# Two of the sixteen blocks of a partition exchange become copies on GpSimd and ScalarE

## The chip, the core and the metric

The kernel runs on one core of one Trainium2 chip. A core has a matrix engine (TensorE, PE in the profile, with its weight loads shown as PEld), three engines for elementwise work (VectorE = DVE, ScalarE = ACT, GpSimd = POOL), and a queue engine (SyncE = SP) which in this kernel does nothing but issue DMA transfers. Each engine takes its instructions strictly in the order in which the program lists them; engines wait for each other through semaphores. The metric is the device time of one execution in microseconds, as a median over runs.

## The reference

The computation is one layer of a transformer block on `x` with 8 batches of 512 rows of 256 values. First comes gated cross-attention, then a gated mixture of experts:

```
x = x + tanh(g_xattn) * (softmax(scale * q k^T) v  Wo + bo)      # 16 heads of 64, 512 keys
        q = layernorm(x) Wq,  k = ctx Wk,  v = ctx Wv
x = x + tanh(g_ffn) * sum over 2 chosen of 8 experts of weight_e * (layernorm(x) We + be)
```

All of it is float32. For every batch and head the attention needs the 512 x 512 matrix of probabilities twice in different orientations: the softmax wants a query's keys along the free dimension, and the product with `v` wants the keys on the partitions.

## The kernel before

**Units and steps.** Heads are taken in pairs (`hp` = 0 to 7), and the 512 queries in four tiles of 128 (`nt` = 0 to 3). One *unit* is (batch, pair, tile). The main loop goes through *steps* of two units, so a pair takes two steps and a batch sixteen: pair `hp` of batch `b` has its first two units in step 16b + 2hp (an even step) and its last two in step 16b + 2hp + 1 (an odd step). There are 128 such steps and some more behind them.

**What a unit goes through.** `scores` (L378, PE) makes 128 queries x 512 keys for each of the two heads in PSUM. `unit_max` (DVE) takes the row maxima (`nm`, L389) and scales them (`nb`, L392, a tiny instruction on 128 x 2 values). `unit_exp` (L401, ACT) writes the exponentials `p` and their sums, `unit_norm` (L410 on DVE, `rs`; L412 on POOL) multiplies them by the reciprocal of the sums. One step later `unit_T` (L425, DVE) transposes `p` in blocks of 32 x 32 into the tile `tt`.

**The exchange.** A transpose of 32 x 32 blocks is not yet a transpose of 128 x 512: the blocks must also move between the four groups of 32 partitions. `exchange` (L433 to L442) does this once per pair, after the last of its four units has been transposed, so in step 2hp + 2 of its batch. It is a list of sixteen DMA transfers, `PAIRS`: block (q, a) goes from partition group `a` of `tt` to partition group `q` of the tile `pt`, 32 partitions x 1024 values (128 KB) each. The first four of the list have q = a: source and target lie in the same 32 partitions. All sixteen go out on SP (in the very last exchange every second one goes out on ACT's queue).

**Who uses it.** `values` (L453, PE, sixteen matmuls `av`) multiplies `pt` by `v` in step 2hp + 5 of the batch. `tt` and `pt` have two buffers each, so the transposes of pair hp + 2, which begin in the same step 2hp + 5, reuse the `tt` of pair hp and wait for its exchange as well.

**The order.** Every function is planned for a step; within a step the scores and maxima of the step come first, and all other functions follow in the order of the list `SCHED["order"]`, which holds for every engine's queue. In it `unit_exp0` comes early, `values` in the second half and `exchange` is next to last. Projections of q, k and v (L357, L367, L347), the output projection (L471) and the expert matmuls are planned for even steps (`at` moves them there), `values` comes in odd steps. So ACT's queue ends an even step with the copies `v`, `k` and `q` out of PSUM (L351, L368, L361) and begins the odd one with the exponentials. POOL also carries `x<-x,tgbo` (L333, a bias on a whole batch tile of x, once per batch), the reciprocal root of the variance (`rstd`, L262), the layer norm of the second half (`xn_f`, L269) and the indirect DMAs of the expert sorting (L611, L733, L793). SP also carries the loads of x, of its transpose and of the context, and the stores and loads of the sorting.

Of the kernel before, what the change touches and what calls it, by code (L numbers as in the profile page):

```python
# [43 lines left out]
        "lt": 2, "lm": 4, "cn": 1, "lc": 2, "lo": 3,  # L44
    },
    "order": [
        "center_q", "sum_q", "ranks_mm", "keep_out", "keep_y", "ln_T", "expert_bias",
        "unit_exp0", "out_proj", "unit_T0", "clear_lists", "logits", "load_lists", "plan4",
        "unit_T1", "places", "ln_apply", "route1", "unit_exp1", "plan1", "plan2", "plan1b",
        "plan3", "load_batch", "sort_setup", "ranks", "experts", "unit_norm0", "values",  # L50
# [9 lines left out]
def kernel(  # L60
# [17 lines left out]
    nc = tc.nc  # L78
# [6 lines left out]
    NT = N // P  # L85
# [102 lines left out]
    def late_setup():  # L188

        nc.sync.dma_start(out=wo_sb, in_=wo.rearrange("(c p) d -> p c d", p=P))  # L190
        nc.sync.dma_start(out=gw_sb, in_=gate_wT.rearrange("(k p) e -> p k e", p=P))
        for k in range(KD):
            nc.sync.dma_start(
                out=we_sb[:, k].rearrange("p (e o) -> p e o", o=O),
                in_=expert_wT[:, :, ts(k, O)].rearrange("e p o -> p e o"),
            )
        nc.gpsimd.memset(eb2, 0.0)
        for t in range(NT):
            nc.sync.dma_start(out=eb2[32 * t : 32 * t + E, ts(t % 2, O)], in_=expert_b)
        nc.scalar.activation(tg, gts, AF.Tanh)  # L200

        nc.gpsimd.tensor_scalar(tgbo, bo_bc, tg[:, 0:1], 1.0, ALU.mult, ALU.mult)

        for e in range(E):
            nc.gpsimd.memset(rev[:, :, e : e + 1], float(E - e))

        for cg in cgs:
            nc.gpsimd.memset(cg, 0.0)
# [104 lines left out]
    def first_q(h):  # L313

        if h == 0:
            qs[0, 0] = qkp.tile([P, N], F32, tag="q", name="q_0_0")
        w = N // 2
        pq = ps_m.tile([P, 512], F32, tag="m", name=f"pq_0_0_{h}")[:, :w]
        for k in range(KD):
            nc.tensor.matmul(  # L320
                pq, lhsT=wq_sb[:, k, ts(0, P)], rhs=xTs["q", 0][:, k, ts(h, w)],
                start=(k == 0), stop=(k == KD - 1),
            )
        nc.scalar.copy(qs[0, 0][:, ts(h, w)], pq)
# [6 lines left out]
    def add_bias(b):  # L331

        nc.gpsimd.tensor_tensor(  # L333
            xs[b], xs[b], tgbo.unsqueeze(1).to_broadcast([P, NT, D]), ALU.add
        )
# [3 lines left out]
    ks, vs, probs, tts, pts, aos = {}, {}, {}, {}, {}, {}  # L339
# [34 lines left out]
    def scores(b, hp, nt):  # L374
        q, kt = qs[b, hp], ks[b, hp]
        sc = ps_s.tile([P, 2, M], F32, tag="s", name=f"sc_{b}_{hp}_{nt}")
        for j in range(2):
            nc.tensor.matmul(  # L378
                sc[:, j, :], lhsT=q[ts(j, HD), ts(nt, P)], rhs=kt[ts(j, HD), :],
                start=True, stop=True,  # L380
            )
        return sc
# [3 lines left out]
    def unit_max(u, sc):  # L386

        nm = small.tile([P, 2], F32, tag="nm", name="nm_%d_%d_%d" % u)
        nc.vector.tensor_reduce(nm, sc, AX.X, ALU.max, negate=True)  # L389
        rstd = lns["q", u[0]][2][:, u[2] : u[2] + 1]  # L390
        nb = small.tile([P, 2], F32, tag="nb", name="nb_%d_%d_%d" % u)
        nc.vector.tensor_scalar(nb, nm, rstd, 1.0, ALU.mult, ALU.mult)  # L392
        maxes[u] = (sc, nb, rstd)
# [36 lines left out]

    PAIRS = [(q, (q + d) % 4 if d % 2 == 0 else q ^ d) for d in (0, 1, 2, 3) for q in (0, 2, 1, 3)]

    def exchange(b, hp):  # L433
        tt = tts.pop((b, hp)).rearrange("p (q k) t l -> p q (k t l)", q=4)
        pt = ptp.tile([P, 4, 2, MT, NT * 32], F32, tag="pt", name=f"pt_{b}_{hp}")
        pts[b, hp] = pt
        last = (b, hp) == (B - 1, NP_ - 1)
        for i, (q, a) in enumerate(PAIRS):
            (nc.scalar if last and i % 2 else nc.sync).dma_start(  # L439
                out=pt[ts(q, 32), a].rearrange("i j r n -> i (j r n)"),  # L440
                in_=tt[ts(a, 32), q],
            )  # L442

    def values(b, hp):
        pt = pts.pop((b, hp))
        v = vs[b, hp // 2]
        ao = aop.tile([P, N], F32, tag="ao", name=f"ao_{b}_{hp}")
        aos[b, hp] = ao
        av = ps_m.tile([P, N], F32, tag="m", name=f"av_{b}_{hp}")
        for mt in range(MT):  # L450
            for j in range(2):
                c = (hp % 2) * P + j * HD
                nc.tensor.matmul(  # L453
                    av[ts(j, HD), :],
                    lhsT=v[:, mt, c : c + HD],
                    rhs=pt[:, :, j, mt, :],
                    start=(mt == 0), stop=(mt == MT - 1),
                )
        nc.scalar.copy(
            ao.rearrange("p (t a l) -> p a t l", a=4, l=32),  # L460
            av.rearrange("p (a t l) -> p a t l", a=4, l=32),
        )
# [457 lines left out]
    for g, (b0, b1) in enumerate(GROUPS):  # L920
# [9 lines left out]
        r = 0  # L930
        for i in range((NTILES[g] + 1) // 2):
            r = G["fe"] + i * num // den
# [29 lines left out]
    def units(s):  # L962
        b, r = divmod(s, NS)
        return [(b, r // 2, 2 * (r % 2) + i) for i in range(2)] if 0 <= b < B else []

    order = {name: i for i, name in enumerate(SCHED["order"])}
    for s in range(max(plan) + 1):
        side = list(plan.get(s, []))
        for i, u in enumerate(units(s)):
            side.append((unit_exp, (i, u)))  # L970
            side.append((unit_norm, (i, u)))
        for i, u in enumerate(units(s - 1)):
            side.append((unit_T, (i, u)))
            if u[2] == NT - 1:
                side.append((exchange, u[:2]))
        scs = [scores(*u) for u in units(s)]
        for u, sc in zip(units(s), scs):
            unit_max(u, sc)
        if s == 0:
            first_q(1)  # L980
            late_setup()
            add_bias(0)
        name = lambda f: f[0].__name__ + (str(f[1][0]) if f[0] in (unit_exp, unit_norm, unit_T) else "")
        for fn, args in sorted(side, key=lambda f: order[name(f)]):
            fn(*args)
# [38 lines left out]
```

## Time and profile before

| | us |
|---|---|
| median of 3 runs | 1049.74 (1046.6 to 1052.07) |
| profiled execution, its own time | 1048.78 |
| its span, first to last instruction | 1046.8 |
| PE busy | 998.3 (95%) |
| DVE busy | 879.9 (84%) |
| ACT busy | 580.0 (55%) |
| POOL busy | 581.9 (56%) |

The span is that of one profiled execution; instruction times below are microseconds from its start. Matmuls are pipelined and their ends are modelled, so a matmul row of 602 ns each does not mean that one takes that long when they follow each other: sixteen `av` take 3.65 us together. A wait is written as the idle time of an engine before an instruction and the thing that ended it. Where an instruction waits for several things, the last of them is named, and sometimes that is only a neighbour that finished at the same moment. The exchange is the group `pt<-tt`: 1016 transfers on SP and 8 on ACT's queue, 134 of the 188.39 MB that the DMA engines move.

### The profile page before, as it was taken

How to read it: one execution, taken by the hardware profiler on the slowest of the kernel's cores; microseconds unless marked ns; L12 is line 12 of the kernel's file. 1: busy time of each engine (PE TensorE's matmuls, PEld its weight loads, DVE VectorE, ACT ScalarE, POOL GpSimd, SP SyncE). 2: the span in 40 equal slices, each digit the busy share in tenths (PEclk: the TensorE clock that was granted, in tenths of full speed). 3: DMA queues.
4: the chain of work that ended last, by engine and by line, in shares of the span. 5: the costliest groups of instructions: out<-in, count | busy, mean ns of one | idle time of the engine just before them, and what ended most of it. 6: DMA issues, size and time to landing. Idle time of an engine off the chain costs nothing.

```text
span 1046.8 us, 14817 instructions
## 1 busy us (share of the span) xinstructions
PE 998.3 (95%) x4024; PEld 492.5 (47%) x4024; DVE 879.9 (84%) x1604; ACT 580.0 (55%) x1379; POOL 581.9 (56%) x771
## 2 busy tenths in 40 slices
PE   8899999999999999989899999999999998898998
PEld 5335344534454444435353445546465543454653
DVE  5998989998999989998899999866686789985467
ACT  4666666566565656575646665665655755552110
POOL 4544546445753466455644665756765457876432
PEclk9999999999999999999999999999999999999999
DMA  7787777769766787576776787787777677889433
GB/s 257 164 202 191 167 177 188 185 146 174 190 158 164 181 192 181 145 179 157 179 175 145 169 194 197 188 205 205 189 192 184 164 146 193 224 226 247 151 118 110
DMA packets 93328, 188.39 MB, mean 180 GB/s; under 512 B 22880, under 2 KB 52992, under 8 KB 93248
## 3 DMA queue, kind: packets, MB, share of 16 engines
q1 hardware_dynamic: 85216, 170.90, 66.5%
q0 software_dynamic: 6816, 14.45, 5.4%
q10 hardware_dynamic: 1216, 2.10, 0.7%
q8 instruction: 34, 0.56, 0.3%
q14 instruction: 46, 0.38, 0.1%
HBM read 33.99 MB, written 19.16 MB: 51 GB/s over the span
## 4 chain that ended last, share of the span: by engine, by line
PE 65%; DVE 17%; DMA 5%; SPq 5%; ACT 4%; issue 3%; DVEq 0%; ACTq 0%; POOL 0%; POOLq 0%
PE sc L378 15%; PE av L453 14%; PE po L471 8%; PE pq L357 8%; DVE nm L389 5%; SPq L439 5%; DMA pt<-tt 5%; DVE tt L425 4%; PE py L761 4%; ACT p L401 4%; PE pv L347 4%; PE pk L367 3%; PE pe L839 3%; DVE nb L392 3%; PE pl L492 1%
## 5 line engine op out<-in xcount | busy, mean ns | idle before, releaser
L401 ACT ACTIVATE p<-sc,nb,rstd_q 128x512 f32<-128x512 f32 x512 | 391.5, 774 | 282.1 <-DVE nb L392 255.4
L412 POOL TENSOR_SCALAR p<-p,rs 128x512 f32<-128x512 f32 x512 | 345.4, 690 | 359.2 <-DVE rs L410 354.4
L389 DVE TENSOR_REDUCE nm<-sc 128x2 f32<-128x1024 f32 x256 | 314.3, 1228 | 67.9 <-PE sc L378 50.5
L425 DVE STREAM_TRANSPOSE tt<-p 128x1024 f32<-128x1024 f32 x256 | 303.9, 1222 | 9.6 <-DMA pt<-tt 7.4
L378 PE MATMUL sc<-k,q 64*128 64x512 f32 x1024 | 261.4, 624 | 19.0 <-ACT p L401 13.4
L453 PE MATMUL av<-pt,v 128*64 128x512 f32 x1024 | 235.5, 602 | 12.3 <-DMA pt<-tt 7.9
L378 PEld LDWEIGHTS sc<-k,q 64*128 64x128 f32 x1024 | 85.9, 186 | 179.7 <-issue 102.1
L453 PEld LDWEIGHTS av<-pt,v 128*64 128x64 f32 x1024 | 70.0, 137 | 170.6 <-issue 145.8
L357 PE MATMUL pq<-xT_q,wq_sb 128*128 128x512 f32 x252 | 120.0, 598 | 3.7 <-DVE wq_sb L309 1.3
L471 PE MATMUL po<-wo_sb,ao 128*128 128x256 f32 x512 | 118.8, 385 | 0.0
L471 PEld LDWEIGHTS po<-wo_sb,ao 128*128 128x128 f32 x512 | 94.7, 190 | 30.6 <-issue 18.2
L392 DVE TENSOR_SCALAR nb<-nm,rstd_q 128x2 f32<-128x2 f32 x256 | 96.4, 376 | 9.2
L401 ACT ACTIVATION_READ_ACCUMULATOR p<-sc,nb,rstd_q 128x1 f32 x512 | 102.0, 199 | 0.0
L357 PEld LDWEIGHTS pq<-xT_q,wq_sb 128*128 128x128 f32 x252 | 47.8, 192 | 67.4 <-issue 57.3
L793 POOL DMA_INDIRECT yg<-ysort,back x48 | 46.6, 971 | 52.3 <-PE xgt L750 19.1
L733 POOL DMA_INDIRECT xg<-xn_d,rows x62 | 61.5, 992 | 15.1 <-issue 13.7
L347 PE MATMUL pv<-wv_sb,ctxT 128*128 128x256 f32 x256 | 68.8, 391 | 0.9 <-issue 0.9
L367 PE MATMUL pk<-ctxT,wk_sb 128*128 128x512 f32 x128 | 66.5, 602 | 2.1 <-DVE x L475 2.1
L761 PE MATMUL py<-we_sb,xgT 128*128 x248 | 57.2, 380 | 3.1 <-DVE x L846 3.1
L347 PEld LDWEIGHTS pv<-wv_sb,ctxT 128*128 128x128 f32 x256 | 45.9, 191 | 23.7 <-issue 18.7
L839 PE MATMUL pe<-we_sb,xT_f 128*128 128x512 f32 x128 | 57.0, 595 | 0.0
L611 POOL DMA_INDIRECT list<-lin,ai x48 | 49.8, 1038 | 10.5 <-issue 10.0
(131 smaller groups left out, 730.7 us busy)
## 6 DMA issues: line engine op xcount, KB each, us to landing
pt<-tt SPq DMA_DIRECT2D x1016, 128.0 KB
ysort<-y SPq DMA_DIRECT2D x30, 256.0 KB
x<-in_x SPq DMA_DIRECT2D x8, 512.0 KB
xT_q<-in_xT SPq DMA_DIRECT2D x7, 512.0 KB
xn_d<-xn_f SPq DMA_DIRECT2D x6, 512.0 KB
x1d<-x SPq DMA_DIRECT2D x5, 512.0 KB
acc<-x1d SPq DMA_DIRECT2D x20, 128.0 KB
out<-acc SPq DMA_DIRECT2D x20, 128.0 KB
```

Source lines behind the costliest of these rows:

```text
L347: nc.tensor.matmul(pv[:, r, :], lhsT=cts[b][:, ts(2 * h + r, P)], rhs=wv_sb[:, ts(g, 2 * P)], start=True, stop=True,)
L357: nc.tensor.matmul(pq, lhsT=wq_sb[:, k, ts(hp, P)], rhs=xTs["q", b][:, k, :], start=(k == 0), stop=(k == KD - 1),)
L367: nc.tensor.matmul(pk, lhsT=wk_sb[:, ts(hp, P)], rhs=cts[b], start=True, stop=True)
L378: nc.tensor.matmul(sc[:, j, :], lhsT=q[ts(j, HD), ts(nt, P)], rhs=kt[ts(j, HD), :], start=True, stop=True,)
L389: nc.vector.tensor_reduce(nm, sc, AX.X, ALU.max, negate=True)
L392: nc.vector.tensor_scalar(nb, nm, rstd, 1.0, ALU.mult, ALU.mult)
L401: nc.scalar.activation(p[:, :, j, :], sc[:, j, :].rearrange("p (q c) -> p q c", q=4), AF.Exp, bias=nb[:, j : j + 1], scale=rstd, accum_out ...
L412: nc.gpsimd.tensor_scalar(p[:, :, j, :], p[:, :, j, :], rs[:, j : j + 1], 1.0, ALU.mult, ALU.mult)
L425: nc.vector.transpose(tts[b, hp][:, :, nt, :], p.rearrange("p q j c -> p (q j c)").rearrange("p (k l) -> p k l", l=32),)
L453: nc.tensor.matmul(av[ts(j, HD), :], lhsT=v[:, mt, c : c + HD], rhs=pt[:, :, j, mt, :], start=(mt == 0), stop=(mt == MT - 1),)
L471: nc.tensor.matmul(po, lhsT=aos[b, c][:, ts(t, P)], rhs=wo_sb[:, c, :], start=(i == 0), stop=(i == HC - 1),)
L761: nc.tensor.matmul(py[:, a, :], lhsT=xt[:, k, a, :], rhs=we_sb[:, k, bass.ds(col[a], O)], start=(k == 0), stop=(k == KD - 1),)
```

## The change

Blocks (0, 0) and (1, 1) of each exchange are no longer transfers. A new function `stay` copies them: GpSimd copies block (1, 1), ScalarE block (0, 0), each 32 partitions x 1024 values. It is planned one step after the exchange (step 2hp + 3 of the batch, an odd step) and stands first in the order, so in ACT's and POOL's queues it precedes everything else of that step. `exchange` keeps the `tt` tile for it. The other fourteen blocks stay as they are.

```diff
     "order": [
-        "center_q", "sum_q", "ranks_mm", ...
+        "stay", "center_q", "sum_q", "ranks_mm", ...
...
+    STAY = [(1,), (0,)]
+
     def exchange(b, hp):
-        tt = tts.pop((b, hp)).rearrange("p (q k) t l -> p q (k t l)", q=4)
+        tt = tts[b, hp].rearrange("p (q k) t l -> p q (k t l)", q=4)
         pt = ptp.tile([P, 4, 2, MT, NT * 32], F32, tag="pt", name=f"pt_{b}_{hp}")
         pts[b, hp] = pt
         last = (b, hp) == (B - 1, NP_ - 1)
         for i, (q, a) in enumerate(PAIRS):
+            if q == a and q in STAY[0] + STAY[1]:
+                continue
             (nc.scalar if last and i % 2 else nc.sync).dma_start(
                 out=pt[ts(q, 32), a].rearrange("i j r n -> i (j r n)"),
                 in_=tt[ts(a, 32), q],
             )
+
+    def stay(b, hp):
+        tt = tts.pop((b, hp)).rearrange("p (q k) t l -> p q (k t l)", q=4)
+        for copy, qs_ in zip((nc.gpsimd.tensor_copy, nc.scalar.copy), STAY):
+            for q in qs_:
+                copy(pts[b, hp][ts(q, 32), q].rearrange("i j r n -> i (j r n)"), tt[ts(q, 32), q])
...
+        for u in units(s - 2):
+            if u[2] == NT - 1:
+                side.append((stay, u[:2]))
```

More of the change, by code (lines that the diff above doesn't have):

```diff
@@ L46 @@
     "order": [
-        "center_q", "sum_q", "ranks_mm", "keep_out", "keep_y", "ln_T", "expert_bias",
+        "stay", "center_q", "sum_q", "ranks_mm", "keep_out", "keep_y", "ln_T", "expert_bias",
         "unit_exp0", "out_proj", "unit_T0", "clear_lists", "logits", "load_lists", "plan4",
```

## Prediction

> **What bounds the kernel now.** I read the page first (engine shares), then the chain that ended last, then the waits of PE, then the timeline around single steps, and last the groups by form for the price of a copy.
>
> ```profile
> PE 998.3 (95%) x4024; PEld 492.5 (47%) x4024; DVE 879.9 (84%) x1604; ACT 580.0 (55%) x1379; POOL 581.9 (56%) x771
> PE 65%; DVE 17%; DMA 5%; SPq 5%; ACT 4%; issue 3%; DVEq 0%; ACTq 0%; POOL 0%; POOLq 0%
> ...
> PE sc L378 <- ACT p L401: 13.4, 13, 2.5
> PE av L453 <- DMA pt<-tt: 7.9, 6, 3.0
> PE av L453 <- DVE nb L392: 2.2, 2, 1.4
> PE av L453 <- DMA li<-list: 1.4, 1, 1.4
> PE av L453 <- DVE nm L389: 0.8, 1, 0.8
> ```
>
> PE is the bound, and it is nearly always at work. The chain's DMA and SPq shares (5% each, some 100 us) look like a large prize, but they count all the time in which the chain runs through the exchange, while PE did other work beside it. What PE really loses before the first `av` is the four `av` rows: 7.9 + 2.2 + 1.4 + 0.8 = 12.3 us, in ten places. The last three rows are the same wait under a neighbour's name, since `av` waits for `pt` alone besides long finished things. In the other 54 pairs the exchange is in time and a shorter one gains nothing.
>
> The ten waits, from the timeline of PE (start of `av`, idle before): 42.3, 0.94; 66.1, 0.41; 133.0, 1.13; 257.2, 0.82; 285.0, 2.21; 354.5, 0.85; 466.9, 1.37; 510.0, 2.98; 596.7, 1.39; 855.9, 0.19.
>
> **Part 1, two transfers fewer.** An undisturbed exchange shows SP's price:
>
> ```profile
> 597.10 10.04 SPq L439 DMA_DIRECT2D pt<-tt  x16
> ...
> 510.02 5.28 PE L453 MATMUL av<-pt,v 128*64 128x512 f32 x16 [2.98 <-DMA pt<-tt]
> ```
>
> 10.04 / 16 = 0.63 us each, so the last block is issued 1.25 us earlier and, other things equal, lands that much earlier. Each of the ten waits shrinks by the smaller of itself and 1.25: 0.94 + 0.41 + 1.13 + 0.82 + 1.25 + 0.85 + 1.25 + 1.25 + 1.25 + 0.19 = 9.3. One is not worth it: behind the `av` of 285.0 the second pair of score matmuls starts at 289.59, 0.19 after the second unit's exponentials end (289.40), because `nb` was held 2.95 us there; PE would wait for ACT instead. That takes the 1.25 down to 0.1: **8.2 us**. For the other nine the scores behind `av` start 0.7 to 2.6 us after the exponentials they need, so the gain passes on. The `av` at 510.0 also takes 5.28 us where others take 3.65, at a granted clock of 0.94 in 490 to 520; if a 1.7 us wait no longer brings that, 1.6 more. I count half: **0.8**. Bounds: nothing if what lands last is set by other traffic, 12.3 + 1.6 = 13.9 if all ten waits vanish. I take the middle, since an issue interval is what the 1.25 is made of.
>
> SP is moved past nothing, it loses 128 issues (80 us). The DMA engines lose 16.8 of 188.39 MB.
>
> **Part 2, the copy on ACT.** 32 x 1024 values. Nearest rows: COPY 128x512 at 588 to 603 ns, 128x256 at 372 to 390; so 0.8 ns a value, and 590 + 512 x 0.8 = 1.0 us, plus a semaphore wait of 0.04. It is queued ahead of the exponentials, after the `q` copy of the even step:
>
> ```profile
> 494.10 0.58 ACT L361 COPY q<-pq 128x512 f32<-128x512 f32 x1 [1.13 <-PE pq L357]
> 496.78 0.78 ACT L401 ACTIVATE p<-sc,nb,rstd_q 128x512 f32<-128x512 f32 x1 [2.09 <-DVE nb L392]
> ...
> 493.52 2.69 POOL L412 TENSOR_SCALAR p<-p,rs 128x512 f32<-128x512 f32 x4 [3.38 <-DVE rs L410]
> 496.19 1.04 POOL L262 TENSOR_TENSOR rstd_f<-ve_f,mhalf 128x4 f32<-128x4 f32 x1
> ...
> 496.43 0.23 DVE L392 TENSOR_SCALAR nb<-nm,rstd_q 128x2 f32<-128x2 f32 x1
> ```
>
> ACT is idle for 2.09 us at this place, waiting for `nb`. The copy's own input (the transposes of the even step) ended at 493.37, before the `q` copy, so it does not wait. Over the 62 odd steps the room is 2.0 or more in 43, about 1.0 to 1.9 in the others but three, where it is 0.6 (121, 186, 636), where the exponentials come 0.45 late; there the next scores have 0.55 or more to spare. **0** on PE; if that cover were gone, 3 x 0.45.
>
> **Part 3, the copy on POOL.** Nearest rows: COPY 128x8 186 ns and CAST 128x40 217 (0.97 ns a value from one to the other), TENSOR_SCALAR 128x256 482 and 128x512 690 (0.82). 690 + 512 x 0.82 = **1.1 us**. Ends: MEMSET 128x512 514 ns, so 0.9; TENSOR_TENSOR 128x1024 2.36. I stay near the copies' own rows, which are the same kind of instruction.
>
> It starts right behind the four L412 of the even step (496.21 above), ahead of `rstd`, L333, L269, L611 and the indirect DMAs. The next L412 come 2.1 to 8 us later, and POOL has the 1.1 us free except once (668.7: 4.84 us with 4.36 of other work, so 0.6 late).
>
> What it hits is `nb`. This row shows it:
>
> ```profile
> 218.39 2.36 POOL L333 TENSOR_TENSOR x<-x,tgbo 128x1024 f32<-128x1024 f32 x1
> ...
> 218.93 1.85 DVE L392 TENSOR_SCALAR nb<-nm,rstd_q 128x2 f32<-128x2 f32 x1
> ...
> 222.58 1.13 PE L378 MATMUL sc<-k,q 64*128 64x512 f32 x4 [0.98 <-ACT p L401]
> ```
>
> A `nb` of 0.23 us takes until the POOL instruction beside it ends (220.75). Laying the `nb` starts of the odd steps over a 1.1 us copy behind the last L412: in nine steps (as above at 496.43) the first `nb` starts 0.2 to 0.3 us into it and both `nb` come 0.72 later; in fifteen the second starts some 0.5 into it and comes 0.45 later; elsewhere none falls into it. Against that, the scores of the next step start 0.62 (nine steps) or 0.25 to 1.6 (fifteen) after the exponentials they need. What exceeds this is 0.08 x 9 and 0.03 to 0.1 x 6, and 1.0 at 669.9, where L333 follows: **2.1 us lost**. That supposes that `nb` gets its turn when the copy ends; in the trace it did at 69 of 71 joins of one L412 with the next, and not at four joins of L269 with L412 (the 2.95 us).
>
> The page SBUF — State Buffer of the Trainium skill, section Who interferes with whom, says that VectorE in a two-port mode and GpSimd exclude each other for a whole instruction and that the first to start wins. It agrees with the 1.85 us and speaks against this change; taken alone, 62 copies of 1.1 us would cost 68 us, while the rows give 2.1 because most `nb` start elsewhere and PE has slack.
>
> The same effect gains where L333 follows L412 directly (218.39, 330.3, 442.1, 556.8): the copy comes first, `nb` slips in at its end, 1.2 us earlier than now, and L333 runs beside the transposes. PE's idle 0.98 before the second scores goes: 4 x 1.0 = **4.0 gained**. If `nb` misses its turn there, 4 x 1.1 lost.
>
> **Part 4, waits added.** The first transpose of pair hp + 2 and `av` wait for ACT and POOL as well, both done two steps before. A semaphore wait on DVE costs 0.1 us (62 x 0.1 beside slack), on PE 0.05; I take **1.0** for all.
>
> **Sum.** 8.2 + 0.8 + 4.0 - 2.1 - 1.0 = 9.9 us. Not all lasts: in 300 to 350, 425 to 450 and 550 to 600 DVE is busy 96% and sets the pace, and the two gains at 330 and 442 and the wait at 597 lie in or beside these. I keep three quarters, 7.5. The profiled execution's own time of 1048.78 becomes 1041.3; it stands 1.0 below the median, so 1042.3 against that.
>
> **Rivals.** *The gain is absorbed* (no measurable change): `av` is earlier, but PE then waits for ACT (already 13.4 us in 13 places) or DVE. For it: DVE at 84%, and the 285.0 case. Against: slack of 0.7 or more behind nine of ten waits. Of 9.9 a quarter stays: 1047. *The landing is not set by the issue*: at 510.0 the last block was issued 4.6 us before `av` could start, against about 2 in quiet places, so other traffic held it; then the change does not do what it says in the worst waits. Left: 0.94 + 0.41 + 1.13 + 0.82 + 0.19 + 4.0 - 3.1 = 4.4, three quarters 3.3: 1046.4. *GpSimd holds `nb` longer* (slower): the same laying over with a copy of 1.4 us costs 5.7 on PE, 1.7 us 11.7, 2.36 us 32; or with 1.1 us and every `nb` that is in the last L412 missing its turn, 12.9. It decides from 1.6 us on, where the cost passes the gain; in the middle of these it is 22 - 9 = 13 slower, 1063, with missed turns alone about 1054.
>
> **How the numbers follow.** The forecast has 0.56, its own range 1035 to 1046. The two absorbed cases together 0.25 (1045 to 1050). GpSimd 0.19 (1052 to 1068). About 0.5%, 5.2 us, is what a measurement can tell from no change: below 1044.5 is most of the forecast's share, 0.53; above 1055 or so are two thirds of the GpSimd case and a few strays, 0.17; the rest 0.30. The range leaves out one in ten at each side: 1033 (more waits vanish than 1.25 each, 13.9 + 4.0 - 1 = 17 off) to 1056.
>
> **What would show it.** Right: 888 `pt<-tt` on SP, exchanges of 8.8 us, the four `av` rows down to 3 or 4 us, an ACT COPY `pt<-tt` near 1.0 and a POOL COPY near 1.1 us, `nb` 1.2 us shorter at 219. Wrong: a POOL COPY over 1.6 us; `nb` over its 96.4 us by more than 20; the row of scores waiting for `p` grown by what the `av` rows lost.

## The result and the profile after

The changed kernel takes 1115.72 us (1111.77 to 1119.45) against 1050.07 us for the one before on the same chip: a ratio of 1.0604, with a 95% interval of 1.0573 to 1.0634. The change costs 65.7 us; 7.5 us of gain were forecast, and the range ended at 1056.

The profiled execution has a span of 1113.5 us. Four lines of its page: the engines, the granted clock in 40 slices of the span (9 is 90% or more), and two groups (busy time and mean ns of one, then the idle time before them and what ended most of it).

```profile
PE 1024.1 (92%) x4024; PEld 497.9 (45%) x4024; DVE 888.9 (80%) x1604; ACT 641.9 (58%) x1443; POOL 648.0 (58%) x835
...
PEclk9899999998999999999999999999999988898999
...
L425 DVE STREAM_TRANSPOSE tt<-p 128x1024 f32<-128x1024 f32 x256 | 306.7, 1226 | 94.9 <-POOL p L412 84.6
...
L452 POOL COPY pt<-tt 32x1024 f32<-32x1024 f32 x64 | 65.8, 1028 | 150.3 <-DMA pt<-tt 73.8
```

Two of VectorE's groups before, for comparison:

```profile
L425 DVE STREAM_TRANSPOSE tt<-p 128x1024 f32<-128x1024 f32 x256 | 303.9, 1222 | 9.6 <-DMA pt<-tt 7.4
...
L392 DVE TENSOR_SCALAR nb<-nm,rstd_q 128x2 f32<-128x2 f32 x256 | 96.4, 376 | 9.2
```

The single instruction is hardly slower: a transpose takes 1226 ns (1222 before), a GpSimd copy 1028; `nb` as a group grew from 96.4 to 107.1 us. What is new is idle time. GpSimd stands idle for 150.3 us in front of its copies, and VectorE for 84.6 us in front of its transposes, waiting for a norm (L412) of GpSimd. PE's own 4024 instructions have become 25.8 us longer (998.3 before) at a mean granted clock of 0.974 instead of 0.993, so part of the loss lies in PE's own rows and not in its waits.

The list of waits shows who waits (engine, tile and line, what ended the wait: us in total, times, longest):

```profile
DVE tt L425 <- POOL p L412: 84.6, 25, 8.5
...
POOL pt L452 <- DMA pt<-tt: 73.8, 12, 11.1
...
PE sc L378 <- ACT p L401: 38.3, 37, 4.3
...
POOL pt L452 <- DMA list<-lin,ai: 7.4, 1, 7.4
```

The first two rows did not exist before. `pt<-tt` in the second is a neighbour's name: the exchange of the same pair is still running when these copies start, so the copy does not wait for it. The last row gives the real one away, an indirect write of the lists. Of the 64 copies 33 start within 0.2 us of the instruction ahead of them; the other 31 stand idle for 148 us together. All 31 lie behind the first indirect DMA of GpSimd (240.73 us).

The first such place, GpSimd's timeline and VectorE's:

```profile
244.23 2.69 POOL L412 TENSOR_SCALAR p<-p,rs 128x512 f32<-128x512 f32 x4 [2.25 <-DVE rs L410]
247.09 1.06 POOL L621 DMA_INDIRECT list<-lin,ai  x1 [0.17 <-issue]
259.23 1.03 POOL L452 COPY pt<-tt 32x1024 f32<-32x1024 f32 x1 [11.08 <-DMA pt<-tt]
260.35 2.02 POOL L412 TENSOR_SCALAR p<-p,rs 128x512 f32<-128x512 f32 x3
```

```profile
251.61 1.22 DVE L389 TENSOR_REDUCE nm<-sc 128x2 f32<-128x1024 f32 x1
...
261.74 2.58 DVE L425 STREAM_TRANSPOSE tt<-p 128x1024 f32<-128x1024 f32 x2 [6.90 <-POOL p L412]
```

GpSimd issues an indirect write of a list (1.06 us), and then the copy, next in its queue, does not start for 11.08 us. Its input was finished at 244.07. The norms stand behind the copy, and the transposes need the norms: VectorE idles 6.90 us, and the maxima, exponentials and scores behind it are late. In the trace the last indirect write ahead of the copy lands at 258.94, 0.3 us before the copy starts. Each such place adds some us that nothing gives back: the last transpose of pair 15 ends at 228.2 us before and 231.4 after, that of pair 31 at 452.0 and 469.3, of pair 47 at 678.6 and 706.9, of pair 63 at 950.7 and 1016.7.

Why the copy waits is in the instruction list of the built program. Around this place it reads (numbers are places in GpSimd's queue; the first buffer number of a name is left out; a list ends with the semaphores, that is the counters, that the instruction waits for):

```
209 L621 DMACopy list_1_156<-lin,ai_2122 16384x1
210 L452 TensorCopy pt_0_2380<-tt_0_2299 32x1024 [waits DMAHW2_49,DMAHW3_49,DMAHW1_49,DMAHW4_49,DMAHW0_49,DMAHW5_49,DMASW1_49,DMAHW6_49,DMASW0_49,DMAHW7_49,PE_49,Pool_49]
211 L412 TensorScalarPtr p_1_2_2411<-p_1_2_2411,rs_1_2_2422 128x4x128 [waits DVE_49,Pool_49]
```

The DMAHW and PE entries are the old users of this `pt` buffer, long done. DMASW0 and DMASW1 are the counters of the indirect DMAs that GpSimd has issued itself since its last copy: here the writes of two lists, which have no byte in common with `pt` or `tt`. Pool_49 is GpSimd's own counter: the copy also waits for the GpSimd instructions ahead of it. Of the 64 copies 38 carry a DMASW entry. It was in the program before any run; my prediction did not ask for it.

### The profile page after: what moved, and what is told of

Same layout as the page of the kernel before. It is cut to its first block, busy times and chain, and to the rows that moved or that the text cites. A ratio compares the mean times of both kernels' runs of the same rounds, so it can differ in the third digit from the quotient of the medians.

```text
span 1113.5 us, 15502 instructions
## 1 busy us (share of the span) xinstructions
PE 1024.1 (92%) x4024; PEld 497.9 (45%) x4024; DVE 888.9 (80%) x1604; ACT 641.9 (58%) x1443; POOL 648.0 (58%) x835
## 5 line engine op out<-in xcount | busy, mean ns | idle before, releaser
L412 POOL TENSOR_SCALAR p<-p,rs 128x512 f32<-128x512 f32 x512 | 344.7, 689 | 214.3 <-DVE rs L410 187.3
L425 DVE STREAM_TRANSPOSE tt<-p 128x1024 f32<-128x1024 f32 x256 | 306.7, 1226 | 94.9 <-POOL p L412 84.6
L378 PE MATMUL sc<-k,q 64*128 64x512 f32 x1024 | 273.4, 642 | 47.6 <-ACT p L401 38.3
L452 POOL COPY pt<-tt 32x1024 f32<-32x1024 f32 x64 | 65.8, 1028 | 150.3 <-DMA pt<-tt 73.8
L357 PE MATMUL pq<-xT_q,wq_sb 128*128 128x512 f32 x252 | 123.8, 615 | 16.2 <-DVE x L485 6.2
L481 PE MATMUL po<-wo_sb,ao 128*128 128x256 f32 x512 | 123.1, 394 | 0.7 <-issue 0.7
L392 DVE TENSOR_SCALAR nb<-nm,rstd_q 128x2 f32<-128x2 f32 x256 | 107.1, 419 | 9.2
L481 PEld LDWEIGHTS po<-wo_sb,ao 128*128 128x128 f32 x512 | 97.3, 195 | 35.9 <-issue 23.5
L452 ACT COPY pt<-tt 32x1024 f32<-32x1024 f32 x64 | 66.6, 1040 | 31.4 <-DVE rs L410 24.9
```

Source lines behind the costliest of these rows:

```text
L357: nc.tensor.matmul(pq, lhsT=wq_sb[:, k, ts(hp, P)], rhs=xTs["q", b][:, k, :], start=(k == 0), stop=(k == KD - 1),)
L378: nc.tensor.matmul(sc[:, j, :], lhsT=q[ts(j, HD), ts(nt, P)], rhs=kt[ts(j, HD), :], start=True, stop=True,)
L412: nc.gpsimd.tensor_scalar(p[:, :, j, :], p[:, :, j, :], rs[:, j : j + 1], 1.0, ALU.mult, ALU.mult)
L425: nc.vector.transpose(tts[b, hp][:, :, nt, :], p.rearrange("p q j c -> p (q j c)").rearrange("p (k l) -> p k l", l=32),)
L452: copy(pts[b, hp][ts(q, 32), q].rearrange("i j r n -> i (j r n)"), tt[ts(q, 32), q])
L481: nc.tensor.matmul(po, lhsT=aos[b, c][:, ts(t, P)], rhs=wo_sb[:, c, :], start=(i == 0), stop=(i == HC - 1),)
```

## The experiments

Two theories could be told apart. *The copy waits for the lists*: the DMASW entries hold GpSimd's queue, and the copy's work matters little. *GpSimd's work*: 66 us of copies on GpSimd, beside which VectorE's `nb` can be held (1.85 us instead of 0.23 at 218.93 before), cost what was lost. All ratios are to the kernel before on the same chip, with 95% intervals; the medians come from several chips, so it is the ratios that compare. "Later" is behind the step's exponentials on ScalarE, "mid step" between the norms of its two units on GpSimd.

| kernel | GpSimd copies | waits for lists | ScalarE copies | transfers | us | ratio |
|---|---|---|---|---|---|---|
| the change | (1,1) | yes | (0,0) | 14 | 1115.72 | 1.0604 [1.0573, 1.0634] |
| e5 | (1,1) | yes | none | 15 | 1116.05 | 1.0634 [1.0585, 1.0683] |
| e3 | 32 x 8 values, partitions 32 to 63 | yes | (0,0) | 15 | 1088.06 | 1.0374 [1.0334, 1.0414] |
| e9 | (1,1), mid step | yes | (0,0), later | 14 | 1071.7 | 1.0227 [1.0179, 1.0274] |
| e11 | (0,0), mid step | no | (1,1), later | 14 | 1061.08 | 1.0078 [1.0047, 1.0108] |
| e10 | (0,0) | no | (1,1), later | 14 | 1054.74 | 1.0074 [1.0049, 1.0100] |
| e1 | (0,0) | no | (1,1) | 14 | 1056.79 | 1.0069 [1.0045, 1.0094] |
| e2 | none | no | both | 14 | 1050.9 | 1.0017 [0.9992, 1.0042] |
| e4 | 32 x 8 values, partitions 0 to 31 | no | (0,0) | 15 | 1050.39 | 1.0006 [0.9984, 1.0027] |
| e8 | none | no | both, later | 14 | 1047.84 | 0.9998 [0.9975, 1.0021] |
| e14 | none | no | (0,0) | 15 | 1048.19 | 0.9982 [0.9953, 1.0010] |
| e13 | none | no | (0,0), later | 15 | 1046.83 | 0.9966 [0.9947, 0.9984] |
| e12 | none | no | (0,0), later | 15 | 1048.46 | 0.9948 [0.9926, 0.9970] |

**e1, the two blocks swapped.** In the program the wait for the lists hangs on the partitions: a GpSimd copy on partitions 32 to 63 has it, the same copy on 0 to 31 has not. So the smallest edit of the change takes the wait away and leaves all the work:

```diff
-    STAY = [(1,), (0,)]
+    STAY = [(0,), (1,)]
```

> GpSimd copies block (0,0) (partitions 0 to 31) and ScalarE block (1,1); all else as in the change. In the program the GpSimd copy then no longer waits for the indirect writes of the lists (L621) that GpSimd issued before it. Theory 'the copy waits for the lists': the 65.7 us are gone, 1038 to 1052; the waits of the transposes for L412 fall from 84.6 us to under 5, the idle time before the copies from 150 to under 15 us. Rival 'GpSimd's work': the copies' 66 us on GpSimd and the port that VectorE shares with them cost what was lost; the time stays at 1100 or more.

1056.79 us, 1.0069. The same place in GpSimd's timeline, and the group of the copies on the page:

```profile
247.92 1.06 POOL L621 DMA_INDIRECT list<-lin,ai  x1 [0.17 <-issue]
248.99 1.05 POOL L452 COPY pt<-tt 32x1024 f32<-32x1024 f32 x1
251.19 2.70 POOL L412 TENSOR_SCALAR p<-p,rs 128x512 f32<-128x512 f32 x4 [1.15 <-DVE rs L410]
```

```profile
L452 POOL COPY pt<-tt 32x1024 f32<-32x1024 f32 x64 | 66.6, 1040 | 0.2
```

The copy follows the indirect write without a gap, and the idle time before all 64 copies is 0.2 us instead of 150.3. VectorE's waits for L412 fall from 84.6 to 6.6 us. Nine tenths of the loss are gone with the wait, the work unchanged: the first theory holds for them, the rival does not. It is not all, though: the kernel is still 0.7% slower than before, 5 us above the range that I had expected, and the 6.6 us are more than the 5 expected.

**e2, both copies on ScalarE.**

```diff
-    STAY = [(1,), (0,)]
+    STAY = [(), (0, 1)]
```

> ScalarE copies both blocks, GpSimd none; fourteen transfers as in the change. Both theories of the loss that lay it on GpSimd say 1035 to 1052, with about 133 us of COPY pt<-tt on ScalarE. Rival 'ScalarE's copy or the fourteen transfers delay PE': still over 1090. Where the first 15 pairs stay 3 us behind the kernel before (231.4 against 228.2 us at the end of pair 15's transposes), that part was not GpSimd's.

1050.9 us, 1.0017: no difference to the kernel before. ScalarE's 133.3 us of copies cost nothing that can be measured, but neither do fourteen transfers gain anything. The last transpose of pair 15 ended at 232.5 us, so the few us at the start were not GpSimd's; with the copies behind the exponentials (e8 below) it ended at 227.7. These are single executions, and the medians of the two kernels do not show the difference.

**e3, the wait without the work.** Block (1,1) is a transfer again. In place of the GpSimd copy stands a tiny one from the same partitions:

```diff
+    scr = single.tile([P, 8], F32, tag="scr", name="scr")
...
-            if q == a and q in STAY[0] + STAY[1]:
+            if q == a and q in STAY[1]:
...
             for q in qs_:
-                copy(pts[b, hp][ts(q, 32), q].rearrange("i j r n -> i (j r n)"), tt[ts(q, 32), q])
+                if copy == nc.gpsimd.tensor_copy:
+                    copy(scr[ts(q, 32)], tt[ts(q, 32), q, 0:8])
+                else:
+                    copy(pts[b, hp][ts(q, 32), q].rearrange("i j r n -> i (j r n)"), tt[ts(q, 32), q])
```

> Block (1,1) goes by transfer again (fifteen in all); in place of the GpSimd copy stands one of 32 x 8 values from the same partitions 32 to 63 into a small spare tile, which waits for the same indirect writes. Theory 'the copy waits for the lists': the work is gone but the loss stays, 1095 to 1120, DVE's waits for L412 60 us or more. Rival 'GpSimd's work': 1045 to 1052, since 64 copies of some 0.2 us are all that is left.

1088.06 us, 1.0374. GpSimd's timeline at the same place, the group on the page, and three rows of the waits:

```profile
243.68 1.06 POOL L625 DMA_INDIRECT list<-lin,ai  x1 [0.17 <-issue]
255.41 0.18 POOL L454 COPY scr<-tt 32x8 f32<-32x8 f32 x1 [10.67 <-DMA list<-lin,ai]
```

```profile
L454 POOL COPY scr<-tt 32x8 f32<-32x8 f32 x64 | 12.0, 188 | 141.8 <-DMA list<-lin,ai 82.1
```

```profile
POOL scr L454 <- DMA list<-lin,ai: 82.1, 17, 10.7
...
POOL scr L454 <- DMA xg<-xn_d,rows: 25.3, 6, 6.8
...
POOL scr L454 <- DMA yg<-ysort,back: 21.0, 6, 4.7
```

A copy of 188 ns waits 141.8 us in all, and since it waits for little else, the trace now names the three kinds of indirect DMA themselves: writes of the lists, and the two gathers. So the wait alone costs 3.7%, some 38 us. I had expected 1095 or more; the further loss with the copy of full length is taken up under e5.

**e4, the same tiny copy without the wait.** From and to partitions 0 to 31; the edit is shown against e3:

```diff
-                    copy(scr[ts(q, 32)], tt[ts(q, 32), q, 0:8])
+                    copy(scr[ts(0, 32)], tt[ts(0, 32), q, 0:8])
```

> The same small copy of 32 x 8 values, at the same place, but from and to partitions 0 to 31, where the program puts no wait for the indirect writes. Fifteen transfers and ScalarE's copy as in e3. Theory 'the copy waits for the lists': 1042 to 1053, next to the kernel before, and 50 us or more below e3. If the place in the queue or the start of a small copy cost the time, it would be as slow as e3.

1050.39 us, 1.0006. The group of the copies:

```profile
L454 POOL COPY scr<-tt 32x8 f32<-32x8 f32 x64 | 12.4, 193 | 0.2
```

Place in the queue, engine, instruction and size are those of e3; the 38 us are the wait (50 or more had been expected, the same miss as in e3). In the instruction list 62 of these 64 copies still wait for GpSimd's own counter (Pool_49) and none for a DMASW counter, so it is the latter that costs the time.

**e5, GpSimd's copy alone.**

```diff
-    STAY = [(1,), (0,)]
+    STAY = [(1,), ()]
```

> Only GpSimd's copy of block (1,1), as in the change; block (0,0) is a transfer again (fifteen), ScalarE copies nothing. Theory 'the copy waits for the lists': nearly all of the loss, 1095 to 1116, DVE's waits for L412 60 us or more. If ScalarE's copy had an own share in the loss beside the wait, it would show as the difference to the 1115.7 of the change: 10 us or more.

1116.05 us, 1.0634: as slow as the whole change. ScalarE's copy has no share in the loss. Beside e3 this also sizes the copy's length where it does wait: 30 copies wait over 1 us in e5 as in e3, and behind each wait the norms are held for 1.03 us more instead of 0.19. 30 x 0.84 = 25 us, against some 27 by the ratios (1.0634 to 1.0374; the two ran on two chips). Without the wait the same work costs 6.6 us (e1 against e4, 1.0069 to 1.0006). That the rest comes from standing at the end of a wait fits in size; it was not isolated.

**e9, the copy in the middle of the step.** The change's own blocks, with the wait, but the function stands behind `unit_norm0` in the order:

```diff
-        "stay", "center_q", ...
+        "center_q", ...
-        ... "experts", "unit_norm0", "values",
+        ... "experts", "unit_norm0", "stay", "values",
```

> The change's own blocks, GpSimd's with its wait for the lists, but both copies stand in the middle of the odd step, on GpSimd between the norms of its first and its second unit, so two norms of 1.4 us and the time between lie between the last indirect write and the copy. Theory 'the copy waits for the lists': the part of the landing that has run by then is not waited for; the idle time before the copies falls from 150 us to 40 to 90 and the time lies at 1065 to 1095. If it were GpSimd's work or its place at the start of the step, 1110 or more in the first case and about 1050 in the second.

1071.7 us, 1.0227. The same place in GpSimd's timeline:

```profile
245.91 1.05 POOL L621 DMA_INDIRECT list<-lin,ai  x1 [0.17 <-issue]
249.18 1.36 POOL L412 TENSOR_SCALAR p<-p,rs 128x512 f32<-128x512 f32 x2 [2.22 <-DMA pt<-tt]
254.16 1.03 POOL L452 COPY pt<-tt 32x1024 f32<-32x1024 f32 x1 [3.61 <-DMA pt<-tt]
```

Two norms and their own wait now pass while the list is on its way, and 3.61 us of waiting are left of 11.08. In all the copies wait 58.2 us instead of 150.3, and the loss falls with it.

**e11, the same place without the wait.** e9 with the blocks swapped as in e1.

> e9 with the blocks swapped as in e1: GpSimd copies block (0,0) without the wait for the lists, between the norms of the two units of the odd step; ScalarE block (1,1) behind the exponentials. Against e9 (1071.7) only the wait is gone: by the theory 'the copy waits for the lists' 1044 to 1056. If 15 us or more of e9's loss came from the copy standing between the norms, it stays at 1062 or more. Against e1 and e10 (1056.8 and 1054.7) only GpSimd's place differs: if their 0.7% is the copy beside the first nb of the step, it falls to 1045 to 1051 here, with nb near 100 us; if the work costs the same anywhere, 1052 to 1058.

1061.08 us, 1.0078. The median lies above the 1044 to 1056 that I had expected, but on a chip where the kernel before takes 1053.97; so I go by the ratio. Against e9's 1.0227 it shows the wait once more. Against e1 and e10 it says that GpSimd's work costs 0.7% to 0.8% at either place, not less as I had hoped. `nb` on the page in e1 and then here:

```profile
L392 DVE TENSOR_SCALAR nb<-nm,rstd_q 128x2 f32<-128x2 f32 x256 | 110.6, 432 | 9.2
```

```profile
L392 DVE TENSOR_SCALAR nb<-nm,rstd_q 128x2 f32<-128x2 f32 x256 | 121.3, 474 | 9.2
```

Against 96.4 us before, `nb` is 14.2 and 24.9 us longer. So the copies do hold VectorE's small instruction; but the time does not follow `nb` (10.7 us more of it, no measurable difference in the ratios; the profiled execution of e11 was its slowest, 1067.6 us). PE's own line in e1 does not settle it either:

```profile
PE 1004.5 (95%) x4024; PEld 491.2 (47%) x4024; DVE 890.7 (84%) x1604; ACT 649.3 (62%) x1443; POOL 648.5 (62%) x835
```

Of a span of 1054.1 us that leaves 49.6 us in which PE idles, against 48.5 before, while its rows take 6.2 us more at an equal granted clock (0.994 and 0.993). How much of the 0.7% is `nb` and how much the norms behind the copy stays open. The Trainium skill's page SBUF — State Buffer, section Who interferes with whom, states a rule that bears on this (GpSimd and VectorE in a two-port mode exclude each other for a whole instruction). The sign agrees with it. Taken for every copy it would have given an estimated 66 us, and a tenth of that was measured.

**e10, ScalarE's copy behind the exponentials.** e1 with `"stay"` behind `"unit_exp1"` in the order; GpSimd's copy keeps its place.

> As e1 (GpSimd block (0,0), ScalarE block (1,1)), but planned behind the exponentials; GpSimd's copy stays where it was in its queue, ScalarE's moves. If e1's 7 us above the kernel before come from GpSimd's copies (they hold nb and delay the norms), it stays at 1052 to 1059; if they come from ScalarE's copy ahead of the exponentials, 1040 to 1050.

1054.74 us, 1.0074, as e1. The 0.7% do not come from the place of ScalarE's copy.

**e8, both copies on ScalarE, behind the exponentials.** e2 with the same move.

> Both copies on ScalarE as in e2, but behind the four exponentials of the step instead of ahead of them. Theory 'the copies ahead of the exponentials eat what the earlier exchange gives': PE's wait of the scores for p, 27.7 us in e2, falls to 16 or less and the time to 1036 to 1046. Theory 'the gain is absorbed whatever the place' (PE, held no longer by the exchange, waits for the exponentials anyway): no change, 1046 to 1054, the scores' wait still over 20 us.

1047.84 us, 0.9998. The place of ScalarE's copies costs nothing that can be seen, and the gain of two transfers fewer does not appear even here. The groups by line show part of where it went: scores and `av` of PE (busy, mean ns | idle before, releasers), before and then in e8, with e8's line of the engines:

```profile
L378 PE MATMUL sc<-k,q 64*128 64x512 f32 x1024 | 261.4, 624 | 19.0 <-ACT p L401 13.4
L453 PE MATMUL av<-pt,v 128*64 128x512 f32 x1024 | 235.5, 602 | 12.3 <-DMA pt<-tt 7.9
```

```profile
L378 PE MATMUL sc<-k,q 64*128 64x512 f32 x1024 | 264.2, 628 | 22.9 <-ACT p L401 22.1 <-ACT q L324 0.5
L463 PE MATMUL av<-pt,v 128*64 128x512 f32 x1024 | 235.5, 602 | 6.7 <-DMA pt<-tt 3.4 <-DMA li<-list 3.4
...
PE 1003.1 (96%) x4024; PEld 492.7 (47%) x4024; DVE 878.5 (84%) x1604; ACT 712.0 (68%) x1507; POOL 581.5 (56%) x771
```

The idle time before `av` falls by 5.6 us (12.3 to 6.7), that before the scores rises by 3.9 (19.0 to 22.9): PE comes to the scores earlier and waits there for the exponentials. But that is not all of it. Over the whole span (1045.7 us) PE idles 42.6 us against 48.5, so some 6 us of waiting did go, and PE's rows take 4.8 us more (1003.1 against 998.3; the scores alone 2.8), at a granted clock of 0.991 against 0.993. Why they do is not shown, and both are single executions. The exchange itself did get shorter. From the end of a pair's transposes to the landing of its last block it takes 13.33 us before in the median, 11.56 in e8.

**e12, e13 and e14, one block on ScalarE, nothing on GpSimd.** Fifteen transfers and one copy:

```diff
-    STAY = [(1,), (0,)]
+    STAY = [(), (0,)]
```

In e12 and e13 (the same kernel on two chips) `"stay"` also moves behind `"unit_exp1"`; e14 leaves it first.

> ScalarE alone copies block (0,0), behind the exponentials; fifteen transfers and nothing on GpSimd: the least of the change. 'The gain is absorbed': 1044 to 1053, no difference. If a gain of some 4 us (half of the 8.2 of two transfers) came through once nothing stands in its way: 1040 to 1046.

> The kernel of e12 once more, on another chip. If its 0.5% is a gain: 0.992 to 0.998 again. If it was chance, as the 0.9998 of e8 and the 1.0006 of e4 suggest: 0.998 to 1.002.

> ScalarE alone copies block (0,0), ahead of the exponentials as in the change; fifteen transfers, nothing on GpSimd. It is e4 without the small copy. If the place of ScalarE's copy matters, it stands 3 us or more above e13 beside it; if not, within 2 us of it. Both theories: 1042 to 1053.

e12 0.9948, e13 0.9966, e14 0.9982. Both intervals of the first kernel end below 1: it is 3 to 6 us faster than the kernel before, 0.3% to 0.5%, the only version that beats both kernels. e14's interval holds no difference, and its median is within 2 us of e13's; whether the place behind the exponentials is needed can't be told. Nor is it shown why one block less in the exchange gains this and two (e8) gain nothing.

## Why the prediction was wrong

**The step that failed is the start of part 3, together with part 4.** The prediction put it so: the copy "starts right behind the four L412 of the even step (496.21 above), ahead of `rstd`, L333, L269, L611 and the indirect DMAs", and "POOL has the 1.1 us free except once". Both are wrong. The function is called one step later, so everything that the even step still had for GpSimd stands ahead of the copy: the reciprocal root, the bias on x, and the indirect write of the list. And part 4, which was to find added waits, asked who waits for the copy (transposes and `av`, put at 1.0 us) and never what the copy waits for on its own engine. Both together are the loss: an instruction that waits for GpSimd's own outstanding transfers, placed directly behind such a transfer, in front of the norms that feed the transposes. e1, e3 and e4 show it: 1.0604 with the wait and 1.0069 without for full copies, 1.0374 and 1.0006 for a copy of 0.19 us.

The row that could have warned was read wrongly. The indirect write is a row of 1.06 us, and I took it as that much of GpSimd's time. The Trainium skill's page Perfetto Trace Analysis, section DMA Instruction — SWDGE (GPSIMD), says that such a row ends when the descriptors are written and not when the data has landed; here the landing came some 11 us behind the row, and whoever waits for it pays that.

**The bound and part 1.** That PE loses 12.3 us in ten waits before `av`, and that two transfers fewer shorten the exchange by 1.25 us, was right: the landing came 1.8 us earlier in e8. The gain of 8.2 us was not: `av` lost 5.6 us of waiting in e8, and no gain was measured. The slack that I read behind each wait (0.7 us or more until the exponentials are late) was read in the kernel before; with the `av` waits gone, the scores wait 3.9 us more. That is the first rival, *the gain is absorbed*; I gave it and its neighbour 0.25, and with GpSimd left out its outcome is what came. Its mechanism, PE waiting for ScalarE instead, is only part of it, since PE's own rows also take 4.8 us more in e8, which no part of the prediction had. What comes through at best is the 0.3% to 0.5% of e12 and e13, with one block. (The neighbour's sum leaves out the wait of 0.85 us at 354.5 without a reason; with it, it gives 1045.8 instead of 1046.4.)

**Part 2.** ScalarE's copy takes 1.04 us, forecast 1.0, and costs nothing measurable (e2, e8, e14), as said.

**Part 3, the sizes.** The copy on GpSimd takes 1.03 us, forecast 1.1. The `nb` hold comes out of the same laying-over as 9 x 0.72 + 15 x 0.45 = 13.2 us of `nb`; e1 measured 14.2. That is at least partly luck, since where other GpSimd work of the even step comes first the copies did not stand where they were laid, and at another place (e11) it was 24.9. And of this only 2.1 us were to reach PE, and the kernels with the copy and without the wait (e1, e10, e11) are 0.7% to 0.8% slow, some 7 us. That PE had less slack than I read is my reading; no run isolates it. The 4.0 us gained where L333 follows the norms do not exist, because L333 comes first there (GpSimd's timeline of the changed kernel, and VectorE's `nb` beside it):

```profile
221.49 2.36 POOL L333 TENSOR_TENSOR x<-x,tgbo 128x1024 f32<-128x1024 f32 x1
223.92 1.03 POOL L452 COPY pt<-tt 32x1024 f32<-32x1024 f32 x1
```

```profile
222.04 1.84 DVE L392 TENSOR_SCALAR nb<-nm,rstd_q 128x2 f32<-128x2 f32 x1
```

`nb` takes 1.84 us there, as the 1.85 before.

**The rival on the slow side** named the right engine and the wrong mechanism. It asked for a copy of 1.6 us or more, and priced the copy's length; the copy was 1.03 us and the wait in front of it cost 38 us. With the wait away, its price for missed turns alone, 1054, is near the 1056.79 of e1, but no run shows that missed turns are what e1 lost.

## What to carry to other kernels

When an instruction is moved to another engine, list what it will wait for in the built program as well as who will wait for it, and put the engine's whole queue around it in order: on GpSimd, which takes its instructions in order and also issues the indirect transfers, a wait on those transfers stopped everything behind it (141.8 us of idle time in e3 before copies of 188 ns). Here the choice of partitions 0 to 31 instead of 32 to 63 for GpSimd's block was worth some 56 us (1.0604 to 1.0069).

A wait that is removed from the bounding engine is not yet a gain: in e8 `av` waits 5.6 us less and the time is the same. That slack read from the trace of before holds for a single event, and not when ten of them move at once, is my reading of it and not shown.

## What the runs showed that I had not expected

The same GpSimd copy waits for GpSimd's outstanding indirect DMAs when it works on partitions 32 to 63 and does not when it works on 0 to 31 (e1 against the change, e4 against e3). This is a wait that the program carries, not a delay of the chip. Instruction lists of variants that were built and not run narrow it down: a copy of block (3,3) has the wait too, a tensor-scalar product in place of the copy and a copy from a weight tile into block (1,1) as well, a memset of block (1,1) and a copy over all 128 partitions have none. A copy from partitions 0 to 31 into block (1,1) has none either, while one from 32 to 63 into block (0,1) has it. So it goes with an input on partitions that do not begin at 0. ScalarE's copies of block (1,1) have none (e1, e2). Why the program is built so stays open.

Behind an indirect write of 1.06 us on the page GpSimd waited 11.08 us until it went on at the first place, and 2.9 to 8.6 us at the others where the copy stood right behind such a write, beside the exchange's transfers, whose queue kept the DMA engines busy for 57% of the span.

PE's granted clock was lower in the versions in which PE idled more: 0.993 with 48.5 us of idle time before, 0.979 with 70.2 in e3, 0.974 with 89.4 in the change; and the same 4024 instructions took 998.3, 1012.8 and 1024.1 us. The change is thus slower by more than PE's idle time alone.
